# A four-layer graph network in one kernel: the way to the first tile reordered, two more lanes at the end, and two tanh as two steps

## The chip, the cores and the metric

The kernel runs on one core of one Trainium2 chip, in one launch. The metric is the device time of an execution in microseconds. Before the change three runs gave 5136.36 to 5138.56 us, with a median of 5137.93.

The core has five engines with a queue of instructions each: PE (TensorE, matrix products into PSUM), DVE (VectorE), ACT (ScalarE), POOL (GpSimd) and SP (SyncE, which here issues DMAs only). ACT's queue issues some DMAs too. [...]

## The reference

64 graphs of 256 nodes with 128 features pass through four layers. Every layer is `x = x + f(relu(layernorm(x)))`; the functions f are, cut to what is computed:

```python
# layer 0: attention of all pairs; W = adj cut into two halves of 128 columns
s1, s2 = h @ W1.T, h @ W2.T                                  # 256 values a node
pre = s1[:, :, None, :] + s2[:, None, :, :] + b_lin          # 64 x 256 x 256 x 256
e = einsum('bije,e->bij', where(pre >= 0, pre, 0.2 * pre), a) + adj
out = sigmoid(softmax(e, axis=2) @ h)
# layer 1: gated sum over neighbours
x_h = elu(h @ Wi + bi)
e = sigmoid(a_tgt[:, :, None] + a_src[:, None, :] + be) * mask(adj)
recv = elu(concat(e @ x_h, x_h * e.sum(-1)) @ Wn + bn)
out = concat(recv, x_h) @ Wm + bm
# layer 2: attention with tanh
A = exp(8 * tanh(h @ q @ (h @ k).T / sqrt(128) / 8)) * adj
out = (A / A.sum(-1)) @ h @ v
# layer 3: five steps of a gated recurrent unit
m = adj @ h                                                  # in and out matrix are both adj
z = sigmoid(concat(m, m) @ w3.T + b3 + h @ u3.T + bu)
r = sigmoid(concat(m, m) @ w4.T + b4 + h @ u3.T + bu)
hv = tanh(concat(m, m) @ w5.T + b5 + (r * h) @ u5.T + b)
h = (1 - z) * h + z * hv
```

The pair term of layer 0 is nearly all of the work: for each graph 256 x 256 pairs of 256 values are formed, passed through a leaky ReLU and summed with the weights a.

## The kernel before, in words

**Tiles.** The 64 graphs form 34 groups, `GROUPS = (1, 1) + (2,) * 30 + (1, 1)`: the first two and the last two groups hold one graph (width W = 256 columns), the others two (W = 512). Groups are counted from 0 here, so the last is 33.

**Layer 0.** `constants0` (L216) sorts the 256 channels by the sign of a: it counts signs with PE (`before`), computes places on DVE, builds the permutation `perm` (four DVE operations), and multiplies adj by it to get `w_p`, the permuted and scaled weights for s1 and s2. From the same pieces come `v2_rep`, `a_win`, `left2`, `left_w`, `adj_t`. `head` (L463) makes the layer norm of a group (`ln_relu`: DVE statistics, four POOL operations that end with `bsh`, two or four ACT operations), transposes it (`h0t`), and makes s1 and its negative s1n; `senders` (L512) makes s2 and, with a vector `bound` that takes a way through DRAM, the term `adj_l`.

The class `Pairs` (L538) then makes the pair tiles `r` of a graph: 32 rows by two channel halves by eight tiles of 128x256, so 512 tiles a graph. Three engines make them: ACT one tile at an instruction (L626), POOL one (L631), DVE four (L614). A batch of eight tiles is summed by PE into `e_ps` (L679) with four matmul instructions, which the trace shows as eight passes of 512 columns. If five batches already wait for PE, a row is "merged": DVE adds the second channel half into the first (L648), and PE gets one batch in place of two. Eleven buffers of r are shared by all. `softmax0` finishes the graph once its last batch is summed.

**Layers 1 to 3.** `layer1` (L759), `layer2` (L843) and `layer3` (L916) are generators: each `yield` ends a step and names the engine of the next. In layer 1 the two tanh of a graph (th_ps, L800) are issued in one step. A step of layer 3 is: `m_ps` (PE), copy to `m_t` (ACT), the products with u3 and w4 into `gate_ps`, tanh (r), `rh2` (DVE), the products with w34, w5 and u5, tanh of both sums (z and the candidate), three DVE operations to the new `hf`, a transpose (PE) and a copy to `hn` (ACT).

**What sets the order.** The order on every engine is written out by a planner while the program is built. A `Model` holds a clock for each engine, and every instruction adds a fixed cost to it. Pieces of work stand in chains (`ahead`, `behind`, `chain12` for layers 1 and 2, `chain3` and `chain4` for layer 3). A chain offers its next step at the latest of: its engine's clock, the end of its last step, a due time which grows by the chain's pace with each step (only while the planning is "paced"), and an earliest time that a step may name. The planner takes what can start first: a chain's step, a batch for PE, or an r tile. The chip's engines then follow these queues whatever their real times are. Layer 3 of groups 0 to 32 stands in `chain3`, one after the other; only the last group has its own lane, `chain4`, with PSUM banks that the pairs use earlier (`Home`, L899).

**The head of the program.** SP loads x of groups 0 and 1 and then most weights. ACT's queue issues adj_n, the columns of a and b_lin, and eight more small loads (L139), then its table load, then the first layer norm.

Of the kernel before, what the change touches and what calls it, by code (L numbers as in the profile page):

```python
# [12 lines left out]
P = 128  # L13
N = 256
# [7 lines left out]
MARGIN = {"pe": 300}  # L22
MEMORY = 7000
# [30 lines left out]
def kernel(ctx: ExitStack, tc: tile.TileContext, ins: dict, out: bass.AP):  # L54
# [87 lines left out]
    def column(name):  # L142

        v = ins[name]
        return fetch(
            [P, v.shape[0] // P], "c_" + name, v.rearrange("(c p) -> p c", p=P), nc.scalar
        )

    order = ctx.enter_context(tc.manual_schedule())
    xts = [load_x(0)]  # L150
    adj_n = fetch([P, 2, N], "adj_n", adj.rearrange("(c p) m -> p c m", p=P), nc.scalar)
    a_col = column("L0_gnn_a")
    blin = column("L0_gnn_b_lin")
    ident = constant([P, P], "ident")
# [47 lines left out]
    bm_bc = fetch([P, P], "bm_bc", ins["L1_gnn_bm"].partition_broadcast(P), nc.scalar)  # L202
    be_bc = fetch([P, 1], "be_bc", ins["L1_gnn_be"].partition_broadcast(P), nc.scalar)
# [12 lines left out]
    def constants0():  # L216
# [10 lines left out]
        yield "dve"  # L227
        sgn, a_abs = col("sgn"), col("a_abs")
        dve(2).tensor_scalar(sgn, a_col, 0.0, None, ALU.is_ge)
        dve(2).scalar_tensor_tensor(a_abs, a_col, -1.0, a_col, ALU.mult, ALU.max)  # L230
        for c in range(2):
            dve(P).tensor_scalar(
                a_rep[:, c, :], a_rep[:, c, :], a_col[:, c : c + 1], None, ALU.mult
            )
# [7 lines left out]


        v2_ps = psum([P, P], "v2_ps")
        for c in range(2):
            mm(
                v2_ps, lhsT=adj_n[:, c, P : 2 * P], rhs=a_rep[:, c, :],
                start=(c == 0), stop=(c == 1),
            )
        yield "dve"  # L250
        bef = constant([P, 3], "bef")
# [57 lines left out]
        odd_all = constant([P, 1], "odd_all")  # L309
        dve(1).tensor_copy(odd_all, p[:, 0:1])  # L310
# [150 lines left out]


# [49 lines left out]
    def senders(b, of, to):  # L512

        h_t = flat(of["h_t"][:, 2 * b : 2 * b + 2, :])
        yield "pe"
        p = psum_h([P, 2, N], "s2_ps")
        for ec in range(2):
            mm(p[:, ec, :], lhsT=w_p[:, 1, bass.ts(ec, P)], rhs=h_t, start=True, stop=True)
        yield "act"
        s2 = ap.tile([P, 2, N], F32, tag="s2", name="s2")  # L520
        act(2 * N).copy(s2, p)
        to["s2"] = s2
# [236 lines left out]
    def layer1(x1):  # L759
# [34 lines left out]
        for b in range(NB):  # L794
# [3 lines left out]
            yield "act"  # L798
            for jc in (1, 0):
                act(N, 1).activation(  # L800
# [379 lines left out]
```

## Time and profile before

| | |
|---|---|
| median of three runs | 5137.93 us |
| the profiled execution: its own time, its span | 5146.74, 5144.9 us |
| instructions of the profiled execution | 152945 |
| first r tile on ACT, last one ends | 23.84, 5033.99 us |
| end of the last batch of pairs (e_ps) | about 5043.2 us |
| first m_ps of the last group's layer 3 | 5097.22 us |
| last operation on DVE (y of the last group) ends | 5142.21 us |
| ACT's r tiles (L626) | 10460, six in 2.2 us |
| POOL's r tiles (L631) | 10200, 475 ns each, spaced 452 |
| DVE's r of four tiles (L614), merges (L648) | 1803, 4896 |
| matmul passes into e_ps (L679) | 27872 |

All times are from the span's start. The profile is of one execution, 8.8 us longer than the median. A table by stage has for each stretch the busy time of PE, PE's weight loads, DVE, ACT and POOL with their instructions in brackets, then the granted PE clock (1.00 is full), the DMA share and GB/s. In a timeline a row is start, duration, engine, line, operation, output<-input, shape and count, and in brackets the idle time before it with what ended it. In a list of waits a row is who waited for whom: total us, times, longest. Ends of matmuls are modelled: a row of PE reaches some 0.2 us past the point at which the next one starts.

### The profile page before, as it was taken

What the parts mean: (1) busy time and instruction counts of PE and PEld (TensorE: products, weight loads), DVE (VectorE), ACT (ScalarE), POOL (GpSimd) and SP (SyncE); (2) the same over time, 40 slices, a digit from 0 to 9 for tenths busy, and PEclk for the clock granted to TensorE, in tenths of its full rate; (3) what the DMA queues carried; (4) which work ended last, traced back from release to release, by engine and by line L of the source; (5) the groups of instructions that cost most, each with busy time, mean ns of one, the idle gap of its engine ahead of it and who ended that gap; (6) DMA issues with size and microseconds to landing.
All of it is one profiled execution on the core that took longest, in us unless ns stands there. A gap on an engine that the chain in (4) does not pass through costs nothing. (4 is left out here: it accounts for less than half of the span.)

```text
span 5144.9 us, 152945 instructions
## 1 busy us (share of the span) xinstructions
PE 5058.0 (98%) x57347; PEld 1988.1 (39%) x57347; DVE 4951.3 (96%) x9664; ACT 5034.1 (98%) x13196; POOL 4862.2 (95%) x10825
## 2 busy tenths in 40 slices
PE   8999999999999999999999999999999999999997
PEld 3334433334343343333344433333333334333343
DVE  7999999999999999999999999999999999999994
ACT  7999999999999999999999999999999999999994
POOL 8999999999999999999999999999999999999991
PEclk9999999999999999999999999999999999999999
DMA  0000000000000000000000000000000000000000
GB/s 20 6 2 5 5 6 6 4 4 6 6 6 6 2 6 6 6 6 2 6 6 6 6 2 6 6 6 6 2 6 6 6 6 5 2 5 4 4 6 6
DMA packets 56028, 28.10 MB, mean 5 GB/s; under 512 B 20337, under 2 KB 55281, under 8 KB 55281
## 3 DMA queue, kind: packets, MB, share of 16 engines
q1 hardware_dynamic: 53168, 17.97, 1.4%
q8 instruction: 449, 7.36, 0.6%
q14 instruction: 299, 2.44, 0.2%
q10 hardware_dynamic: 2112, 0.33, 0.0%
HBM read 9.84 MB, written 8.45 MB: 4 GB/s over the span
## 5 line engine op out<-in xcount | busy, mean ns | idle before, releaser
L631 POOL TENSOR_SCALAR r<-s,s1n 128x256 f32<-128x256 f32 x10200 | 4612.8, 475 | 81.0 <-PE e_ps L679 21.9
L626 ACT ACTIVATE r<-s_act,s 128x256 f32<-128x256 f32 x9948 | 4489.0, 1312 | 2.6 <-PE e_ps L679 2.6
L679 PE MATMUL e_ps<-r,a_win 128*32 128x512 f32 x27872 | 3330.9, 594 | 5.6 <-POOL r L631 2.3
L614 DVE TENSOR_TENSOR r<-s_dve,s1n 128x1024 f32<-128x1024 f32 x1803 | 2093.9, 1211 | 4.7
L648 DVE SCALAR_TENSOR_TENSOR r<-s_dve,s1n,r 128x256 f32<-128x256 f32 x4896 | 2002.3, 472 | 1.0 <-POOL r L631 1.0
L679 PEld LDWEIGHTS e_ps<-r,a_win 128*32 128x32 f32 x27872 | 958.1, 110 | 1734.4 <-issue 1255.6
L443 ACT ACTIVATE h<-x,bsh,brs 128x128 f32<-128x128 f32 x384 | 320.5, 1344 | 2.1 <-POOL bsh L437 2.1
L626 ACT ACTIVATE r<-s,s 128x256 f32<-128x256 f32 x512 | 311.1, 1207 | 0.0
L106 PE MATMUL m_ps<-adj_t,hn 128*32 128x256 f32 x4096 | 261.0, 388 | 3.1 <-ACT hn L974 3.0
L932 ACT COPY m_t<-m_ps 128x512 f32<-128x512 f32 (+1 forms) x170 | 229.4, 1349 | 15.8 <-PE m_ps L106 15.7
L951 ACT ACTIVATE gate_ps<-gate_ps,bz 128x512 f32<-128x512 f32 (+1 forms) x170 | 236.6, 1392 | 7.0 <-PE gate_ps L106 6.9
L953 ACT ACTIVATE hv_ps<-hv_ps,bh 128x512 f32<-128x512 f32 (+1 forms) x170 | 234.2, 1378 | 2.4 <-PE hv_ps L106 2.4
L938 ACT ACTIVATE m_ps<-gate_ps,br 128x512 f32<-128x512 f32 (+1 forms) x170 | 226.2, 1331 | 8.9 <-PE gate_ps L106 8.9
L974 ACT COPY hn<-hn_ps 128x512 f32<-128x512 f32 (+1 forms) x136 | 186.6, 1372 | 17.8 <-PE hn_ps L113 17.8
L106 PEld LDWEIGHTS m_ps<-adj_t,hn 128*32 128x32 f32 x4096 | 141.2, 112 | 132.0 <-issue 44.8
L106 PE MATMUL gate_ps<-m_t,t_w_w 128*32 128x512 f32 (+1 forms) x1360 | 173.3, 572 | 9.7 <-ACT m_t L932 9.0
L106 PE MATMUL gate_ps<-m_t,w_t 128*32 128x512 f32 (+1 forms) x1360 | 175.0, 569 | 5.0 <-ACT m_ps L938 5.0
L106 PE MATMUL hv_ps<-m_t,t_w_w 128*32 128x512 f32 (+1 forms) x1360 | 174.6, 567 | 0.0
L106 PE MATMUL hv_ps<-rh,u_th 128*32 128x512 f32 (+1 forms) x1360 | 174.5, 567 | 0.0
L432 POOL TENSOR_SCALAR bve<-bmv 128x4 f32<-128x4 f32 (+1 forms) x136 | 26.2, 193 | 128.7 <-DVE bmv L427 119.9
L106 PE MATMUL s_ps<-h0t,w_p 128*32 128x256 f32 (+1 forms) x1568 | 139.4, 449 | 5.4 <-ACT s1n L482 2.8
L106 PE MATMUL gate_ps<-hf,u_t 128*32 128x512 f32 (+1 forms) x1088 | 143.9, 574 | 0.0
(206 smaller groups left out, 5211.6 us busy)
## 6 DMA issues: line engine op xcount, KB each, us to landing
xt<-in_x_dram SPq DMA_DIRECT2D x30, 256.0 KB
out_dram<-y SPq DMA_DIRECT2D x30, 256.0 KB
row<-rows SPq DMA_DIRECT2D x128, 0.5 KB
xt<-in_x_dram SPq DMA_DIRECT2D x4, 128.0 KB
out_dram<-y SPq DMA_DIRECT2D x4, 128.0 KB
bound<-row SPq DMA_DIRECT2D x30, 2.0 KB
raw_L_gnn_w_w<-in_L_gnn_w_w_dram SPq DMA_DIRECT2D x3, 128.0 KB
adj_n<-in_adj_dram ACTq DMA_DIRECT2D x1, 256.0 KB
```

Source lines behind the costliest of these rows:

```text
L106: nc.tensor.matmul(out[bass.ts(c, 32), :], lhsT=lhsT[:, bass.ts(c, 32)], rhs=rhs, **flags)
L443: act(P, 2, 1).activation(h[:, g, :], xt[:, g, :], AF.Relu, bias=shift[:, g : g + 1], scale=rstd[:, g : g + 1],)
L614: nc.vector.tensor_tensor(r[:, 2 * g2 : 2 * g2 + 2, :, :], s2[:, ec : ec + 1, :].unsqueeze(1).to_broadcast([P, 2, 2, N]), self.s1n_v[:, ec ...
L626: nc.scalar.activation(r[:, g, ic, :], s2[:, ec, :], AF.Relu, bias=s1[:, ec, i : i + 1])
L631: nc.gpsimd.tensor_scalar(r[:, g, ic, :], s2[:, ec, :], FLT_MAX, s1n[:, ec, i : i + 1], ALU.min, ALU.max,)
L648: nc.vector.scalar_tensor_tensor(r[:, g, ic, :], self.own("dve")[:, 1, :], self.of["s1n"][:, 1, i : i + 1], r[:, g, ic, :], ALU.max, ALU.add,)
L679: nc.tensor.matmul(self.e_ps[bass.ts(g, 32), :, :].rearrange("p a b -> p (a b)"), lhsT=a_win[:, batch["ec"], 31 - t : 63 - t], rhs=flat(r[ ...
L932: act(W).copy(m_t, m_ps)
L938: act(W, 1).activation(t_r, g_ps, AF.Tanh, bias=br, scale=0.5)
L951: act(W, 1).activation(t_z, g_ps, AF.Tanh, bias=bz, scale=0.5)
L953: act(W, 1).activation(cand, hv_ps, AF.Tanh, bias=bh)
L974: act(W).copy(hn, tp)
```

## The change

**Head.** The column of a is ACT's first DMA and adj_n its second; all other columns, bm_bc and be_bc go to SP, b_lin as SP's second. A memset and a tanh on one element are put ahead of everything on DVE and ACT. In `constants0` the products that the first tile doesn't need (v2, a_rep, odd) move behind w_p; w_p's halves are made and copied one by one, the s2 half first; the products of b_lin come ahead of w_p's. The first group has its own head, `first_head`: s2 and s1 in one block of products, s1n on DVE, s1 on ACT. `constants0` and the first layer norm name an earliest time (LANDS).

**Planning.** The first graph isn't paced, and when its pairs begin, the planner's clocks are all set to at least ACT's.

**Layer 1.** Each of the two tanh of a graph is a step of its own, so that the planner may put other work between.

**End.** Group 32's layer 3 has the lane chain4, with the two banks that the last group had; group 33's has a new lane chain5 with three banks (two of e_ps, one of ps_h). Both may begin in the planning only when no pairs are left. In group 33 (`early`) the w5 product comes before the first tanh, u5 before w34, and the candidate's tanh before z's.

```diff
+LANDS = 3400
...
-    def column(name):
+    def column(name, queue=nc.sync):
         v = ins[name]
-        return fetch(
-            [P, v.shape[0] // P], "c_" + name, v.rearrange("(c p) -> p c", p=P), nc.scalar
-        )
+        return fetch([P, v.shape[0] // P], "c_" + name, v.rearrange("(c p) -> p c", p=P), queue)
...
     xts = [load_x(0)]
+    a_col = column("L0_gnn_a", nc.scalar)
     adj_n = fetch([P, 2, N], "adj_n", adj.rearrange("(c p) m -> p c m", p=P), nc.scalar)
-    a_col = column("L0_gnn_a")
     blin = column("L0_gnn_b_lin")
+    table = constant([P, 1], "table")
+    nc.vector.memset(table, 0.0)
+    nc.scalar.activation(table, table, AF.Tanh)
...
-    bm_bc = fetch([P, P], "bm_bc", ins["L1_gnn_bm"].partition_broadcast(P), nc.scalar)
-    be_bc = fetch([P, 1], "be_bc", ins["L1_gnn_be"].partition_broadcast(P), nc.scalar)
+    bm_bc = fetch([P, P], "bm_bc", ins["L1_gnn_bm"].partition_broadcast(P))
+    be_bc = fetch([P, 1], "be_bc", ins["L1_gnn_be"].partition_broadcast(P))
...
-        yield "dve"
+        yield "dve", None, LANDS + 500
         sgn, a_abs = col("sgn"), col("a_abs")
         dve(2).tensor_scalar(sgn, a_col, 0.0, None, ALU.is_ge)
-        dve(2).scalar_tensor_tensor(a_abs, a_col, -1.0, a_col, ALU.mult, ALU.max)
-        for c in range(2):
-            dve(P).tensor_scalar(
-                a_rep[:, c, :], a_rep[:, c, :], a_col[:, c : c + 1], None, ALU.mult
-            )
...
-        v2_ps = psum([P, P], "v2_ps")
-        for c in range(2):
-            mm(
-                v2_ps, lhsT=adj_n[:, c, P : 2 * P], rhs=a_rep[:, c, :],
-                start=(c == 0), stop=(c == 1),
-            )
-        yield "dve"
+        yield "dve"
+        dve(2).scalar_tensor_tensor(a_abs, a_col, -1.0, a_col, ALU.mult, ALU.max)
...
         yield "pe"
+        b_ps = psum([P, 2], "blin_ps")
+        for c in range(2):
+            for src in range(2):
+                mm(
+                    b_ps[:, c : c + 1], lhsT=perm[:, src, c, :], rhs=blin[:, src : src + 1],
+                    start=(src == 0), stop=(src == 1),
+                )
         p = psum([P, 2, N], "w_p_ps")
-        for half in range(2):
+        for half in (1, 0):
...
-        yield "act"
-        act(2 * N).copy(w_p, p)
-        counts["w_p"] += 1
+        yield "dve"
+        dve(2).tensor_copy(blin_p, b_ps)
+        dve(2).tensor_scalar(blin_n, b_ps, -1.0, None, ALU.mult)
+        for half in (1, 0):
+            yield "act"
+            act(N).copy(w_p[:, half, :], p[:, half, :])
+        counts["w_p"] += 2
+        yield "dve"
+        for c in range(2):
+            dve(P).tensor_scalar(
+                a_rep[:, c, :], a_rep[:, c, :], a_col[:, c : c + 1], None, ALU.mult
+            )
+        yield "pe"
+        v2_ps = psum([P, P], "v2_ps")
+        for c in range(2):
+            mm(
+                v2_ps, lhsT=adj_n[:, c, P : 2 * P], rhs=a_rep[:, c, :],
+                start=(c == 0), stop=(c == 1),
+            )
         yield "dve"
         dve(P).tensor_copy(v2_rep, v2_ps)
...
         yield "pe"
-        p = psum([P, 4], "odd_ps")
-        mm(p[:, 0:1], lhsT=ones, rhs=odd, start=True, stop=True)
-        for c in range(2):
-            for src in range(2):
-                mm(
-                    p[:, 1 + c : 2 + c], lhsT=perm[:, src, c, :], rhs=blin[:, src : src + 1],
-                    start=(src == 0), stop=(src == 1),
-                )
-        yield "dve"
-        dve(2).tensor_copy(blin_p, p[:, 1:3])
-        dve(2).tensor_scalar(blin_n, p[:, 1:3], -1.0, None, ALU.mult)
-        counts["w_p"] += 1
+        p = psum([P, 1], "odd_ps")
+        mm(p, lhsT=ones, rhs=odd, start=True, stop=True)
+        yield "dve"
...
-    def ln_relu(space, xt, tag, ln, when=None):
...
-                yield "dve", when
+                yield "dve", when, at
...
+    def first_head(xt, to, snd):
+        G, _, W = sizes(xt)
+        h = yield from ln_relu(ap, xt, "h0", "h0", at=LANDS)
+        h_t = yield from transpose_blocks(ap, h, "h0t", psum_h)
+        to.update(h=h, h_t=h_t)
+        yield "pe", lambda: counts["w_p"] > 1
+        s2_ps, s1_ps = psum_h([P, 2, N], "s2_ps"), psum_a([P, 2, W], "s1_ps")
+        for half, p in ((1, s2_ps), (0, s1_ps)):
+            for ec in range(2):
+                mm(
+                    p[:, ec, :], lhsT=w_p[:, half, bass.ts(ec, P)], rhs=flat(h_t),
+                    start=True, stop=True,
+                )
+        yield "dve"
+        s1n = ap.tile([P, 2, W], F32, tag="s1n", name="s1n")
+        for ec in range(2):
+            dve(W, 1).tensor_scalar(
+                s1n[:, ec, :], s1_ps[:, ec, :], -1.0, blin_n[:, ec : ec + 1], ALU.mult, ALU.add
+            )
+        yield "act"
+        s2 = ap.tile([P, 2, N], F32, tag="s2", name="s2")
+        act(2 * N).copy(s2, s2_ps)
+        s1 = ap.tile([P, 2, W], F32, tag="s1", name="s1")
+        for ec in range(2):
+            act(W, 1).activation(
+                s1[:, ec, :], s1_ps[:, ec, :], AF.Identity, bias=blin_p[:, ec : ec + 1]
+            )
+        to.update(s1=s1, s1n=s1n)
+        snd["s2"] = s2
...
+        if "s2" not in to:
+            yield "pe"
+            p = psum_h([P, 2, N], "s2_ps")
+            for ec in range(2):
+                mm(p[:, ec, :], lhsT=w_p[:, 1, bass.ts(ec, P)], rhs=h_t, start=True, stop=True)
+            yield "act"
+            s2 = ap.tile([P, 2, N], F32, tag="s2", name="s2")
+            act(2 * N).copy(s2, p)
+            to["s2"] = s2
...
-            yield "act"
             for jc in (1, 0):
+                yield "act"
                 act(N, 1).activation(
                     th_ps[:, jc, :], th_ps[:, 0, :], AF.Tanh,
                     bias=a_src[:, 2 * b + jc : 2 * b + jc + 1], scale=0.5,
...
-        def __init__(self, aside):
-            self.aside = aside
-        def bank(self, shape, name, odd):
-            if not self.aside:
+        LAST = ((ps_e, "e"), (ps_e, "e"), (ps_h, "ps_h"))
+        LAST_BUT_ONE = ((ps_d, "s2_dve"), (ps_c, "s2_act"))
+        def __init__(self, g):
+            self.banks = {len(GROUPS) - 1: self.LAST, len(GROUPS) - 2: self.LAST_BUT_ONE}.get(g)
+            self.taken = 0
+        def bank(self, shape, name):
+            if not self.banks:
                 return psum(shape, name)
-            space, tag = ((ps_d, "s2_dve"), (ps_c, "s2_act"))[odd % 2]
+            space, tag = self.banks[self.taken % len(self.banks)]
+            self.taken += 1
...
             act(W).copy(m_t, m_ps)
             yield "pe"
             mm(g_ps, lhsT=ws["w4_w"], rhs=m_t, start=False, stop=True)
+            early = home.banks is home.LAST
+            if early:
+                hv_ps = home.bank([P, W], "hv3_ps")
+                mm(hv_ps, lhsT=ws["w5_w"], rhs=m_t, start=True, stop=False)
...
             yield "pe"
+            if early:
+                mm(hv_ps, lhsT=u5_th, rhs=rh2, start=False, stop=True)
             mm(
                 g_ps, lhsT=w34_t, rhs=m_t, start=False, stop=True, skip_group_check=True
             )
-            hv_ps = home.bank([P, W], "hv3_ps", step)
-            mm(hv_ps, lhsT=ws["w5_w"], rhs=m_t, start=True, stop=False)
-            mm(hv_ps, lhsT=u5_th, rhs=rh2, start=False, stop=True)
-            yield "act"
+            if not early:
+                hv_ps = home.bank([P, W], "hv3_ps")
+                mm(hv_ps, lhsT=ws["w5_w"], rhs=m_t, start=True, stop=False)
+                mm(hv_ps, lhsT=u5_th, rhs=rh2, start=False, stop=True)
             t_z, cand = g_ps, hv_ps
-            act(W, 1).activation(t_z, g_ps, AF.Tanh, bias=bz, scale=0.5)
-            yield "act"
-            act(W, 1).activation(cand, hv_ps, AF.Tanh, bias=bh)
+            for of_z in (not early, early):
+                yield "act"
+                if of_z:
+                    act(W, 1).activation(t_z, g_ps, AF.Tanh, bias=bz, scale=0.5)
+                else:
+                    act(W, 1).activation(cand, hv_ps, AF.Tanh, bias=bh)
...
-        last = g == len(GROUPS) - 1
-        (chain4 if last else chain3).add(last_rest(g, x3, hn, h_t, Home(last)))
+        lane = {len(GROUPS) - 1: chain5, len(GROUPS) - 2: chain4}.get(g, chain3)
+        lane.add(last_rest(g, x3, hn, h_t, Home(g)))
     def last_rest(g, x3, hn, h_t, home):
+        if home.banks:
+            yield "pe", lambda: n == len(graphs) and not (making or doing or multiplying)
         y = yield from layer3(x3, hn, h_t, home)
         nc.sync.dma_start(out=of_group(out, g), in_=y)
         counts["out"] += 1
...
-    chain4 = Chain(2400)
-    chains = [ahead, behind, chain3, chain12, chain4]
+    chain4, chain5 = Chain(2400), Chain(2400)
+    chains = [ahead, behind, chain5, chain3, chain12, chain4]
...
-    ahead.add(head(xts[0], made[0]))
+    ahead.add(first_head(xts[0], made[0], sent[0]))
...
-        paced = n < len(graphs) - 2
+        paced = 0 < n < len(graphs) - 2
         if not making and n < len(graphs) and "s2" in sent[n]:
             g, b = graphs[n]
             making.append(Pairs(g, b, made[g], sent[n]))
+            if n == 0:
+                model.t = {e: max(t, model.t["act"]) for e, t in model.t.items()}
             multiplying.append(making[0])
```

More of the change, by code (lines that the diff above doesn't have):

```diff
@@ L296, in constants0 @@
         yield "pe"
-        p = psum([P, 4], "odd_ps")
-        mm(p[:, 0:1], lhsT=ones, rhs=odd, start=True, stop=True)
-        for c in range(2):
-            for src in range(2):
-                mm(
-                    p[:, 1 + c : 2 + c], lhsT=perm[:, src, c, :], rhs=blin[:, src : src + 1],
-                    start=(src == 0), stop=(src == 1),
-                )
+        p = psum([P, 1], "odd_ps")
+        mm(p, lhsT=ones, rhs=odd, start=True, stop=True)
         yield "dve"
-        dve(2).tensor_copy(blin_p, p[:, 1:3])
-        dve(2).tensor_scalar(blin_n, p[:, 1:3], -1.0, None, ALU.mult)
-        counts["w_p"] += 1
         odd_all = constant([P, 1], "odd_all")
-        dve(1).tensor_copy(odd_all, p[:, 0:1])
+        dve(1).tensor_copy(odd_all, p)
         left, left_n, left_nb = col("left"), col("left_n"), col("left_nb")
@@ L411, in constants1, with ln_relu @@
                 dve(1).tensor_scalar(t, t, scale, None, ALU.mult)
-    def ln_relu(space, xt, tag, ln, when=None):
+    def ln_relu(space, xt, tag, ln, when=None, at=None):
         G = xt.shape[1]
@@ L514, in senders @@
         h_t = flat(of["h_t"][:, 2 * b : 2 * b + 2, :])
[L515 to L518, printed above, removed]
-        yield "act"
-        s2 = ap.tile([P, 2, N], F32, tag="s2", name="s2")
-        act(2 * N).copy(s2, p)
-        to["s2"] = s2
+        if "s2" not in to:
[7 more added lines that the diff above has]
+            to["s2"] = s2
         if "bound" not in of:
@@ L899 @@
     class Home:
-        def __init__(self, aside):
-            self.aside = aside
-        def bank(self, shape, name, odd):
-            if not self.aside:
+        LAST = ((ps_e, "e"), (ps_e, "e"), (ps_h, "ps_h"))
[5 more added lines that the diff above has]
+            if not self.banks:
                 return psum(shape, name)
-            space, tag = ((ps_d, "s2_dve"), (ps_c, "s2_act"))[odd % 2]
+            space, tag = self.banks[self.taken % len(self.banks)]
+            self.taken += 1
             return space.tile(shape, F32, tag=tag, name=name)
         def tile(self, W, tag, name, bufs=1):
-            if not self.aside:
+            if not self.banks:
                 return bp.tile([P, W], F32, tag=tag, name=name, bufs=bufs)
@@ L920, in layer3 @@
             yield "pe"
-            m_ps = home.bank([P, W], "m_ps", step)
+            m_ps = home.bank([P, W], "m_ps")
             for b in range(NB):
@@ L927, in layer3 @@
                     )
-            g_ps = home.bank([P, W], "gate_ps", step + 1)
+            g_ps = home.bank([P, W], "gate_ps")
             mm(g_ps, lhsT=u3_t, rhs=hf, start=True, stop=False)
@@ L945, in layer3 @@
             )
-            hv_ps = home.bank([P, W], "hv3_ps", step)
-            mm(hv_ps, lhsT=ws["w5_w"], rhs=m_t, start=True, stop=False)
-            mm(hv_ps, lhsT=u5_th, rhs=rh2, start=False, stop=True)
-            yield "act"
+            if not early:
+                hv_ps = home.bank([P, W], "hv3_ps")
+                mm(hv_ps, lhsT=ws["w5_w"], rhs=m_t, start=True, stop=False)
+                mm(hv_ps, lhsT=u5_th, rhs=rh2, start=False, stop=True)
             t_z, cand = g_ps, hv_ps
-            act(W, 1).activation(t_z, g_ps, AF.Tanh, bias=bz, scale=0.5)
-            yield "act"
-            act(W, 1).activation(cand, hv_ps, AF.Tanh, bias=bh)
+            for of_z in (not early, early):
[4 more added lines that the diff above has]
+                    act(W, 1).activation(cand, hv_ps, AF.Tanh, bias=bh)
             yield "dve"
@@ L967, in layer3 @@
                 yield "pe"
-                tp = home.bank([P, W], "hn_ps", step)
+                tp = home.bank([P, W], "hn_ps")
                 turn()
@@ L976, in layer3 @@
         yield "pe"
-        tp = home.bank([P, W], "y_ps", step)
+        tp = home.bank([P, W], "y_ps")
         turn()
```

## The prediction, made before the changed kernel was run

> **What bounds the kernel now.** First the page's busy shares, then busy time by stage.
>
> ```profile
> PE 5058.0 (98%) x57347; PEld 1988.1 (39%) x57347; DVE 4951.3 (96%) x9664; ACT 5034.1 (98%) x13196; POOL 4862.2 (95%) x10825
> ```
>
> ```profile
> core 0: us, PE busy (x) PEld busy (x) DVE busy (x) ACT busy (x) POOL busy (x), PEclk, DMA share, GB/s
> 0.00:10.00 10.00, 1.61 (x56) 1.19 (x56) 5.29 (x30) 0.00 (x0) 3.07 (x17) 1.00 0.49 130
> 10.00:20.00 10.00, 5.81 (x90) 2.65 (x90) 1.35 (x10) 3.96 (x7) 0.00 (x0) 1.00 0.34 89
> ...
> 40.00:60.00 20.00, 17.71 (x131) 5.10 (x131) 16.82 (x37) 10.31 (x30) 19.65 (x44) 1.00 0.00 1
> ...
> 3000.00:4000.00 1000.00, 990.42 (x11112) 376.40 (x11108) 981.67 (x1950) 999.53 (x2617) 973.01 (x2161) 1.00 0.02 5
> ...
> 5100.00:5145.00 45.00, 30.94 (x442) 13.72 (x434) 15.43 (x37) 15.80 (x39) 0.00 (x0) 0.95 0.03 8
> ```
>
> The middle is full on four engines, and fullest on ACT: between 62 and 5030 us it idles 6.9 us. So the time is ACT's list from its first r to its last (23.84 to 5033.99), plus the head before, the idle time inside, and a tail of 110 us. What can move is at both ends. The head and the first graph, from the timeline and the waits between 23 and 62 us:
>
> ```profile
> 5.24 0.17 DVE L229 TENSOR_SCALAR sgn<-c_L_gnn_a 128x2 f32<-128x2 f32 x1 [0.85 <-DMA c_L_gnn_a<-in_L_gnn_a_dram]
> 10.49 1.28 ACT L443 ACT_TABLE_LOAD   x1 [10.49 <-DMA c_L_gnn_w_b<-in_L_gnn_w_b_dram]
> 13.12 3.64 PE L106 MATMUL w_p_ps<-perm,adj_n 128*32 128x256 f32 x32
> 23.84 1.71 ACT L626 ACTIVATE r<-s,s 128x256 f32<-128x256 f32 x4
> ```
>
> ```profile
> ACT h L443 <- POOL bsh L437: 9.7, 1, 9.7
> DVE adj_t L348 <- PE adj_t_ps L113: 7.6, 1, 7.6
> ACT rows L501 <- PE bound_ps L496: 5.1, 1, 5.1
> ```
>
> ACT issues ten DMAs until 10.45 before it loads its table; h comes at 11.79, and PE's w_p products stand behind h's transposes. Then ACT stops twice, 14.8 us in all, at instructions queued too early for PE and POOL. The tail, from PE's timeline (W = 256):
>
> ```profile
> 5115.61 1.07 PE L106 MATMUL m_ps<-adj_t,hn 128*32 128x256 f32 x16
> 5118.22 0.61 PE L106 MATMUL gate_ps<-m_t,t_w_w 128*32 128x256 f32 x8
> 5124.81 1.07 PE L106 MATMUL m_ps<-adj_t,hn 128*32 128x256 f32 x16
> 5133.64 1.81 PE L106 MATMUL m_ps<-adj_t,hn 128*32 128x256 f32 x16 [0.46 <-ACT hn L974]
> ```
>
> Two lanes of layer 3 alternate with a period of 9.20 us; no engine is full, latency sets the end.
>
> [...] granted clock 0.50 from 5052 to 5058, and 32 m_ps passes take 3.64 there against 1.91. [...]
>
> **Part 1, the way to the first tile.** Ten DMA issues leave ACT (0.33 to 0.49 us each) for SP. SP's list ended at 12.84, now near 17; its next use (row) is at 32.7, the next data needed from it (bm_bc) at DVE 47.0: hidden. The table load now runs near 1.7 to 3.0, before x lands (bst at 3.90). The new memset and one-element tanh (0.1 and about 0.2) hide there too.
> The column a: landed 4.0 us after its issue, behind the 256 KB of adj. Now first: earliest it is harmless (bst ends 4.39), latest 0.72 + 4.0 = 4.7. I take sgn at 4.45 (was 5.24). Then: PE's counts, 0.8 to bef (5.52 to 6.32), so bef 5.4; bef to the last perm, 2.8 (6.32 to 9.11), so 8.2 (adj_n, second on ACT, and blin, second on SP, are issued by 1.7 and have landed); blin product 0.5; w_p products 3.4 at the cold rate of the row above: 12.1. POOL's 1.4 us for rstd and h on ACT (0.88) end near 7.3, under that. The two transposes 0.6, h0t copy and its wait 0.6: 13.3. s products, 32 passes as one block, 1.9 warm (3.6 cold): 15.2. s1 by two ACTIVATEs 0.8, beside it s1n by two DVE operations (0.48 and 0.40, off ACT): first r on ACT and POOL at about 15.8, against 23.84: **-8.0**. Ends: -9.9 (a early, PE warm) to -6.0 (PE cold through s). DVE's first half comes later, after v_rep, a_win and s_dve, 17.7 against 24.57. The products for v2, odd, left and adj_t move behind the first tile; they were on the way only through PE's and DVE's order, and PE has room there (it waited 18.6 us for POOL's r between 23 and 62).
>
> **Part 2, the first graph's order.** The planner's four clocks are set equal at the first pair and the first graph isn't paced. In the changed program's queues ACT has 53 r before rows and 40 more before the next h (read from the order of the changed program's instructions on each engine); POOL has 71 r before that h's statistics. From 15.8, at 0.367 us an r on ACT (six in 2.2) and 0.4525 on POOL: POOL reaches bsh at 15.8+32.1+1.4 = 49.3, ACT reaches h at 15.8+35.5 = 51.3: no wait where 9.7 was. rows at 35.8; PE's bound product waits for DVE's left_w, about 36.4: 0.6 to 2.5 us where 5.1 was. adj_t's product, for which DVE stood 7.6, now stands behind 18 batches on PE and its copy behind 19 halves on DVE. I leave 2.3 of 14.8: **-12.5**, from -14 to -4 (an unforeseen stop of 10).
>
> **Part 3, the two tanh.** Same instructions; between them now stand mostly one to five r. ACT's r count is 10460 before and after, so its list is equally long: **0**. POOL has 20 r fewer, DVE 88 merges fewer and 27 halves more (-34.5+31.6 at 0.392 and 1.17), PE 11 batches more (+9.5 at 0.86): PE's passes at their measured rates (0.1075 for 512 columns) fill about 95% of the phase, so there is room. Bound: ACT idle from 3 less to 6 more.
>
> **Part 4, end of the pairs.** Before, 24 passes of the last batches stood behind group 31's transposes, m_ps and u3, and e_ps ended at 5043.2, 9.2 after ACT's last r. Now the last r come 2.0 after group 31's r-tanh, PE follows with w34, w5, u5 (2.6) and 40 passes (4.3), and group 31's next step starts after them: 5.5 to 7.2 after the last r: **-3**.
>
> **Part 5, tail.** From e_ps's end to the last group's first m_ps was 54.0 (5043.2 to 5097.2). Group 32's five steps now run in this stretch with group 31's last three. PE's list there is 20 (31) + 17 (32) + 10.5 (33) = 47.5 us warm, against about 33 plus 6.6 lost to the halved clock. Following the queues with the measured durations (us after e_ps's end, before in brackets): x1 8.4 (8.5); h_t's transposes 14.6 (15.7, cold); xh 19.6 (17.0), behind group 31's m_ps and u3; th 25.6 (22.0), behind its w34, w5, u5; rc 31.6 (30.2); x2 36.6 (34.9); g 42.6 (39.7), behind another such block; pm 47.3 (45.3); first m_ps 54.5 (54.0). Waits that this misses can add 2.5; I take 55. Then the last group is alone. A step: 9.20, less 1.1 (w4 behind the other lane, 5117.12 to 5118.22), less 1.0 (cand behind its hn copy), less 0.5 (u5 no longer behind w34 and w5): 6.6. [...] the last step before shows the price, w4 ends 3.5 instead of 2.0 after m_ps starts: 8.1 at worst, I take 7.4; the first step also waits for group 32's y, 8.0. Last step, y and output DMA: 10.1 (2.7 of it after y, as now). 55+8.0+3x7.4+10.1 = 95.3 against 101.7: **-6**, from -10 to 0.
>
> Sum: -8.0-12.5+0-3-6 = -29.5 on a span of 5144.9 (execution 5146.74, 8.8 above the median 5137.93): span 5115.4, median **5108**.
>
> **Rivals.**
> Tail gained nothing (13%): group 32's lane delays layers 1 and 2 of the last group to 58 and every step runs at the halved clock: 58+8.7+24.3+10.8 = 101.8. For it: PE's 47.5 of 55 us; against: three drops of clock in that stretch become rarer. -23.5: 5114.
> The first graph stalls elsewhere (10%): one in-order wait of 10 us, at rows or for an r buffer. For it: left_w now comes after 15 DVE halves; against: both queues worked out above. 5118.
> Better (10%): middle -3, warm steps, a early: 5098.
> Slower (3%): the single psum_a bank is held longer by the split tanh (up to five r, 1.8 us), and rsum or the next layer-1 product stops PE and then ACT in every graph. From 29.5/64 = 0.46 us a graph nothing is left; at 0.65 it is +12: 5150. Against: ACT idles 6.9 us in 62 graphs now, e_t made DVE wait only 9.0 in all.
> The parts don't do it (4%): a lands as late as before and the stops move: gain under 10.
> The forecast itself, 5102 to 5114: 60%.
> About 0.2% (10 us) can be told from no change. So faster 0.93, same 0.04, slower 0.03; range 5097 to 5121.
>
> **What would show it.** Table load before 3.5 and w_p products ahead of h's transposes; first r near 16; ACT busy over 90% from 20 to 60; POOL's bsh before ACT's h; ACT idle in the middle under 13 us; last r about 5013; e_ps's end within 7.5 us of it; last five steps at 6.6 to 8.1[...]. Wrong if s products run cold and a lands late, if rows stops ACT, or if e_t or rsum appear as waits in every graph.

## The result and the profile after

The changed kernel takes **5100.43 us** (median of six executions, 5098.04 to 5115.52), the kernel before beside it 5136.39 (six, 5134.57 to 5138.56): a ratio of **0.9934, 95% interval 0.9921 to 0.9947**, or 36 us less. Forecast were 5108 and a range of 5097 to 5121. The profiled execution is the slowest of the six: 5115.52, span 5112.6, against 5144.9 before.

Profiled executions of one kernel differ by some 10 us, 0.2% (an r starts 356.8 ns after the last in after and 356.1 in again, and the pairs take 4996.2 and 4985.9 us), so stretches are compared at one rate here: the profiles of before and after both have 356.8.

The page of the changed kernel, the line of busy shares:

```profile
PE 5042.1 (99%) x57435; PEld 1964.8 (38%) x57435; DVE 4950.0 (97%) x9606; ACT 5029.2 (98%) x13196; POOL 4876.0 (95%) x10805
```

Its busy time by stage (columns as before: stretch, its length, then PE, PEld, DVE, ACT, POOL, clock, DMA share, GB/s):

```profile
40.00:60.00 20.00, 19.86 (x170) 6.83 (x166) 19.93 (x30) 19.41 (x54) 18.34 (x41) 1.00 0.01 1
...
3000.00:4000.00 1000.00, 993.24 (x11316) 389.19 (x11312) 983.08 (x1914) 1000.00 (x2625) 978.20 (x2162) 1.00 0.02 5
```

The first graph is now as full as the middle: ACT has 19.41 of 20 us between 40 and 60, where it had 10.31. Its timeline at the head:

```profile
1.76 1.28 ACT L155 ACT_TABLE_LOAD   x1 [1.76 <-issue]
3.46 0.15 DVE L231 TENSOR_SCALAR sgn<-c_L_gnn_a 128x2 f32<-128x2 f32 x1
7.51 3.63 PE L107 MATMUL w_p_ps<-perm,adj_n 128*32 128x256 f32 x32
15.28 0.84 ACT L494 ACTIVATE s<-s_ps,blin_p 128x256 f32<-128x256 f32 x2 [1.25 <-DVE s1n L486]
16.01 1.70 ACT L664 ACTIVATE r<-s,s 128x256 f32<-128x256 f32 x4
```

The table load, the column a and the w_p products come first as worked out, and the first r starts at 16.01 instead of 23.84. The waits of ACT between 15 and 62 us (total, times, longest) have shrunk from 9.7 and 5.1 to this:

```profile
ACT s L494 <- DVE s1n L486: 1.2, 1, 1.2
ACT rows L538 <- PE bound_ps L533: 0.7, 2, 0.5
ACT h0t L465 <- PE h0t_ps L114: 0.3, 1, 0.3
```

PE's timeline of the last group's lone steps:

```profile
5067.54 1.07 PE L107 MATMUL m_ps<-adj_t,h 128*32 128x256 f32 x16
5075.85 1.93 PE L107 MATMUL m_ps<-adj_t,hn 128*32 128x256 f32 x16 [0.46 <-ACT hn L1027]
5084.50 1.86 PE L107 MATMUL m_ps<-adj_t,hn 128*32 128x256 f32 x16 [0.46 <-ACT hn L1027]
5093.00 1.93 PE L107 MATMUL m_ps<-adj_t,hn 128*32 128x256 f32 x16 [0.46 <-ACT hn L1027]
5101.60 1.90 PE L107 MATMUL m_ps<-adj_t,hn 128*32 128x256 f32 x16 [0.46 <-ACT hn L1027]
```

The period is 8.3 to 8.65 us where 7.4 was taken: four of the five m_ps run at half the clock (1.9 against 1.07; the granted clock is 0.68 on the mean from 5074 to 5106). In three stretches the two profiles stand so; "pairs" runs from ACT's first r to the last pass into e_ps, "tail" from there to the end of the span:

| us | before | after | predicted for after |
|---|---|---|---|
| first r on ACT | 23.84 | 16.01 | 15.8 |
| pairs | 5019.5 | 4996.2 | 5004 |
| tail | 101.6 | 100.4 | 95.3 |

The pairs gained 23 where 15.5 were forecast (parts 2, 3 and 4 together), the tail 1 where 6 were. Two questions for the chip: what made the extra 8 us, and is the tail really worth nothing?

### The profile page after: what moved, and what is told of

It reads as the page before. It is cut to its first block, busy times and chain, and to the rows that moved or that the text cites. A ratio compares the mean times of both kernels' runs of the same rounds, so it can differ in the third digit from the quotient of the medians.

```text
span 5112.6 us, 153009 instructions
## 1 busy us (share of the span) xinstructions
PE 5042.1 (99%) x57435; PEld 1964.8 (38%) x57435; DVE 4950.0 (97%) x9606; ACT 5029.2 (98%) x13196; POOL 4876.0 (95%) x10805
## 5 line engine op out<-in xcount | busy, mean ns | idle before, releaser
L664 ACT ACTIVATE r<-s_act,s 128x256 f32<-128x256 f32 x9948 | 4611.6, 1577 | 0.9 <-PE e_ps L717 0.8
L686 DVE SCALAR_TENSOR_TENSOR r<-s_dve,s1n,r 128x256 f32<-128x256 f32 x4808 | 1964.2, 472 | 0.5 <-ACT r L664 0.4
L664 ACT ACTIVATE r<-s,s 128x256 f32<-128x256 f32 x512 | 365.4, 1609 | 0.0
L1006 ACT ACTIVATE hv_ps<-hv_ps,bh 128x512 f32<-128x512 f32 (+1 forms) x170 | 278.2, 1636 | 9.1 <-PE hv_ps L107 9.1
L1004 ACT ACTIVATE gate_ps<-gate_ps,bz 128x512 f32<-128x512 f32 (+1 forms) x170 | 281.8, 1658 | 4.0 <-PE gate_ps L107 4.0
L976 ACT COPY m_t<-m_ps 128x512 f32<-128x512 f32 (+1 forms) x170 | 270.5, 1591 | 13.5 <-PE m_ps L107 13.3
L986 ACT ACTIVATE m_ps<-gate_ps,br 128x512 f32<-128x512 f32 (+1 forms) x170 | 267.7, 1575 | 9.6 <-PE gate_ps L107 9.4
L838 ACT ACTIVATE th_ps<-th_ps,a_src 128x256 f32<-128x256 f32 x128 | 202.5, 1582 | 1.5 <-PE th_ps L107 1.5
L107 PE MATMUL gate_ps<-m_t,t_w_w 128*32 128x512 f32 (+1 forms) x1360 | 176.5, 578 | 10.3 <-ACT m_t L976 9.2
L741 ACT ACTIVATE pm<-e_ps,nmax 128x256 f32<-128x256 f32 x128 | 185.1, 1446 | 0.5 <-DVE nmax L732 0.5
L771 ACT ACTIVATE e_ps<-e_ps,rh 128x128 f32<-128x128 f32 x128 | 166.6, 1302 | 0.2 <-PE e_ps L107 0.2
```

Source lines behind the costliest of these rows:

```text
L107: nc.tensor.matmul(out[bass.ts(c, 32), :], lhsT=lhsT[:, bass.ts(c, 32)], rhs=rhs, **flags)
L664: nc.scalar.activation(r[:, g, ic, :], s2[:, ec, :], AF.Relu, bias=s1[:, ec, i : i + 1])
L686: nc.vector.scalar_tensor_tensor(r[:, g, ic, :], self.own("dve")[:, 1, :], self.of["s1n"][:, 1, i : i + 1], r[:, g, ic, :], ALU.max, ALU.add,)
L976: act(W).copy(m_t, m_ps)
L986: act(W, 1).activation(t_r, g_ps, AF.Tanh, bias=br, scale=0.5)
L1004: act(W, 1).activation(t_z, g_ps, AF.Tanh, bias=bz, scale=0.5)
```

## The experiments

Each run is compared with the kernel before in the same set of runs (5146.3, 5146.4 and 5146.5 us in the three sets, each on a chip of its own: again to split_alone, warm to act_dmas, plan_off to rates).

| run | median us | ratio to before, 95% | first r | pairs | tail |
|---|---|---|---|---|---|
| again | 5107.5 | 0.992 [0.9907, 0.9934] | 15.80 | 4985.9 * | 93.7 * |
| join | 5117.1 | 0.994 [0.9926, 0.9953] | 15.51 | 5004.5 | 99.8 |
| pair_l2 | 5119.1 | 0.9948 [0.9935, 0.996] | 16.15 | 5006.1 | 95.0 |
| split_alone | 5135.4 | 0.9978 [0.997, 0.9986] | 23.91 | 5008.6 | 102.5 |
| warm | 5106.3 | 0.9919 [0.9905, 0.9932] | 16.35 | 4986.5 * | 93.5 * |
| lanes_old | 5116.1 | 0.9938 [0.9925, 0.995] | 15.76 | 4985.8 * | 102.6 * |
| clocks_old | 5105.8 | 0.9917 [0.9904, 0.9931] | 16.03 | 4985.3 * | 94.0 * |
| act_dmas | 5112.0 | 0.993 [0.9917, 0.9944] | 16.13 | 4996.1 | 97.2 |
| plan_off | 5113.3 | 0.9936 [0.9924, 0.9949] | 15.65 | 4997.8 | 99.0 |
| both | 5107.3 | 0.9924 [0.991, 0.9938] | 15.92 | 4996.1 | 93.4 |
| rates_act | 5066.9 | 0.9846 [0.9832, 0.9859] | 16.22 | 4953.0 | 96.4 |
| rates | 5078.9 | 0.987 [0.9856, 0.9883] | 15.90 | 4974.0 | 87.6 |

The columns from "first r" on are of the profiled execution. A star marks 356.1 ns a r; times 1.002, 4985.9 is 4996.0, the value of after. With that the pairs of after, again, warm, act_dmas and both, which have the same queues there but for the first microseconds, agree within 0.7 us, so differences of some 1 us and more can be read.

### What the split of the two tanh is worth

Between before and after ACT's number of r is the same (10460), so its instructions should take equally long. They don't, and a view that the prediction didn't use says where. The groups of ACT's instructions by line and form give, behind the bar, busy time and the mean length of one record in ns. The kernel before:

```profile
L626 ACT ACTIVATE r<-s_act,s 128x256 f32<-128x256 f32 x9948 | 4489.0, 1312 | 2.6 <-PE e_ps L679 2.6
L800 ACT ACTIVATE th_ps<-th_ps,a_src 128x256 f32<-128x256 f32 x128 | 98.0, 766 | 2.6 <-PE th_ps L106 0.4
```

The changed kernel:

```profile
L664 ACT ACTIVATE r<-s_act,s 128x256 f32<-128x256 f32 x9948 | 4611.6, 1577 | 0.9 <-PE e_ps L717 0.8
L838 ACT ACTIVATE th_ps<-th_ps,a_src 128x256 f32<-128x256 f32 x128 | 202.5, 1582 | 1.5 <-PE th_ps L107 1.5
```

An r's record is 1312 or 1577 ns long though r start 357 ns apart: the records overlap, up to eight at a time in both traces. A tanh of before has 766 on the mean, because half of them have 450, near the shortest tanh of all (433). That is the second of each pair. It writes the half of th_ps that the first reads, and the semaphore that it waits on is ACT's own: in all 64 pairs it starts 32 to 34 ns after the first one's end, and in these 32 to 34 ns no record of ACT is under way. The timeline of the kernel before shows one place:

```profile
1799.62 0.95 ACT L800 ACTIVATE th_ps<-th_ps,a_src 128x256 f32<-128x256 f32 x2
1800.48 0.83 ACT L626 ACTIVATE r<-s_act,s 128x256 f32<-128x256 f32 x2
```

0.86 us from the first tanh to the r behind the second, where two starts take 0.71. By the ends, which count when starts bunch, the second tanh of a pair ends 482 ns (median) after the first in the kernel before; in the changed kernel a tanh ends 339 ns after the instruction ahead of it. 64 x 0.143 = 9 us. Of each 0.143 only 0.033 is idle time in the profile: the first tanh's record runs until just before the second starts.

Theory A is this; its rival B is that the planner's other order made the 8 us. Three kernels beside the changed one, on one chip:

```diff
 # join: the changed kernel, with
             for jc in (1, 0):
-                yield "act"
                 act(N, 1).activation(
+            # (one yield "act" ahead of the loop, as before)
 # pair_l2: the changed kernel, with
             act(2 * N, table=1).activation(s_ps, s_ps, AF.Tanh, scale=INV_SQRT_D / 8.0)
-            yield "act"
             act(2 * N, table=1).activation(s_ps, s_ps, AF.Exp, scale=8.0)
 # split_alone: the kernel before, with the two lines of the split and nothing else
```

> The changed kernel once more, as the measure for the runs beside it. Both theories: 5098 to 5102 us, 36 under the kernel before; ACT from its first to its last r 4989 us; second tanh of a graph ends 0.34 us after the instruction before it.

> The changed kernel with layer 1's two tanh of a graph as one step again. Theory A (the second tanh overwrites what the first reads, so ACT waits for its own first tanh to end[...]: in the kernel before the second ends 0.482 us after the first, in the changed kernel 0.339 after the instruction ahead of it): 64 x 0.143 = 9 us slower than the changed kernel, about 5109; the ACT phase from first to last r 9 us longer, and all of it in the step from the first tanh to the second. Theory B (the 7 us that the middle gained come from the planner's different order, the split itself is worth nothing, as predicted): within 3 us of the changed kernel, of either sign, and no such step in the ends.

> The changed kernel with layer 2's tanh and exp of a graph (both in place on the same PSUM tile) put one right behind the other, where r stood between them. Theory A: another 64 dependent pairs[...]: 64 x 0.14 = 9 us slower than the changed kernel, the exp ending about 0.63 us after the tanh where it took 0.487. Theory B: within 3 us, either sign.

> The kernel before with the two tanh as two steps, and nothing else of the change. Theory A: 9 us faster than the kernel before, about 5127, ACT from first to last r 5001 instead of 5010. Theory B: within 3 us of the kernel before.

Measured: join is 9.5 us slower than the changed kernel beside it, pair_l2 11.6 slower, and split_alone 10.9 faster than the kernel before, with an interval that leaves 1 out. The intervals of join and again overlap a little; the pairs at one rate don't leave the question open, with 5004.5 in join against 4996.2. The tanh in join and in split_alone:

```profile
L838 ACT ACTIVATE th_ps<-th_ps,a_src 128x256 f32<-128x256 f32 x128 | 103.5, 809 | 2.8 <-PE th_ps L107 0.7
L800 ACT ACTIVATE th_ps<-th_ps,a_src 128x256 f32<-128x256 f32 x128 | 196.8, 1538 | 1.5 <-PE th_ps L106 1.5
```

Up to ACT's last r, the sum over the ends into the tanh is 51.9 us in join and 43.0 in the changed kernel (52.0 before, 43.3 in split_alone), so the step itself is worth 8.7 to 8.9. The stretch from ACT's first to its last r moved by less than the 9 us expected: 7.5 more in join, 6.4 less in split_alone (5010.1 to 5003.7). In split_alone another 4.5 of the 10.9 come after the last r, where e_ps ends 4.9 us behind it in place of 9.4; so the step is shown, but that the totals come so near to 9 is partly luck. The layer-2 pair, which was never part of the change, shows the same mark. pair_l2:

```profile
L909 ACT ACTIVATE s_ps<-s_ps 128x512 f32<-128x512 f32 x64 | 78.0, 1219 | 0.5 <-PE s_ps L107 0.5
L910 ACT ACTIVATE s_ps<-s_ps 128x512 f32<-128x512 f32 x64 | 37.2, 582 | 2.0
```

and the changed kernel, where r stand between the two:

```profile
L911 ACT ACTIVATE s_ps<-s_ps 128x512 f32<-128x512 f32 x64 | 97.7, 1527 | 0.0
```

The exp's record falls to 582 ns, its end comes 614 ns (median) behind the tanh's instead of 487, and the sum of these steps grows by 8.0 us. Theory A is confirmed by taking the split away, by adding it alone, and by the same fault made elsewhere; B expected under 3. Of pair_l2's 11.6 some 3 are not explained by it; ACT also has 8 r more there (10468), an estimated 2.9 us at 0.365 each.

### What the tail is worth: the clock

again, the changed kernel once more, had a tail of 93.7 us. PE's timeline there:

```profile
5057.03 1.07 PE L107 MATMUL m_ps<-adj_t,h 128*32 128x256 f32 x16
5065.08 1.07 PE L107 MATMUL m_ps<-adj_t,hn 128*32 128x256 f32 x16 [0.46 <-ACT hn L1027]
5071.99 1.07 PE L107 MATMUL m_ps<-adj_t,hn 128*32 128x256 f32 x16 [0.46 <-ACT hn L1027]
5078.89 1.07 PE L107 MATMUL m_ps<-adj_t,hn 128*32 128x256 f32 x16 [0.46 <-ACT hn L1027]
```

Same queues, steps of 6.9 us. Up to the first m_ps, 55.3 us behind e_ps in both, the two tails agree within 0.02 us; what differs is the granted clock, 0.68 from 5074 to 5090 in after and 1.00 in again. Is it a cause, or does it follow? Within a step ACT's and DVE's records have the same length in both traces (0.37 and 0.45, 0.42 us). From m_ps to rh, where PE's products ran at half the clock (m_ps 1.86 against 1.07), the slow step of 5084.50 takes 4.15 us and the fast one of 5071.99 takes 2.80; from rh to the next hn 3.92 and 3.68. So the time is lost in PE's own products, 1.35 us of it. warm puts products into the gaps: PE stands idle for 1.7 us before a transpose in after and again:

```diff
             if early:
+                for _ in range(3):       # behind w34; one more between w5 and u5
+                    mm(psum([P, W], "warm"), lhsT=ones, rhs=m_t, start=True, stop=True)
```

> The changed kernel with four idle matmuls of 128x256 in each step of the last group (one between w5 and u5, three behind w34; their results are read by nobody). Theory A (the five lone steps take 8.6 us where PE's clock drops in the gap of 1.7 us before the transposes, and 6.9 where it doesn't, as two executions of the changed kernel show): clock 1.0 to the end, steps of 6.9 us, tail 93 to 94 us in every execution, 3 to 4 us under the changed kernel's median and 7 under its execution with a tail of 100.4. Theory B (the steps are latency of ACT and DVE, and the clock only follows): tail unchanged or longer by up to 2 us, since the idle matmuls stand ahead of u5 and of the transposes.

In after the granted clock fell four times in these steps, twice in such a gap (5074.39 and 5091.45) and twice 0.1 us behind the start of m_ps (5084.63 and 5101.69).

The same view of warm:

```profile
5066.20 1.07 PE L107 MATMUL m_ps<-adj_t,hn 128*32 128x256 f32 x16 [0.46 <-ACT hn L1031]
5073.05 1.07 PE L107 MATMUL m_ps<-adj_t,hn 128*32 128x256 f32 x16 [0.46 <-ACT hn L1031]
5079.89 1.07 PE L107 MATMUL m_ps<-adj_t,hn 128*32 128x256 f32 x16 [0.46 <-ACT hn L1031]
```

Steps of 6.85 us with the idle matmuls in them, 0.30 us of idle time before a transpose, and a tail of 93.5 here and of 93.4 in both, at the other rate. Since again reached 93.7 without them, one such trace proves little; the count over all traces says more. Of the last four m_ps of the last group 11 of 28 ran at half the clock, for part of their length at least, in the seven traces with these lanes and no idle matmuls (after 4, again 0, join 3, pair_l2 1, clocks_old 0, act_dmas 2, plan_off 1), and 1 of 16 in the four with them. That one is in rates_act, so "in every execution" was too much:

```profile
5034.13 1.94 PE L107 MATMUL m_ps<-adj_t,hn 128*32 128x256 f32 x16 [0.46 <-ACT hn L1032]
5042.26 1.07 PE L107 MATMUL m_ps<-adj_t,hn 128*32 128x256 f32 x16 [0.46 <-ACT hn L1032]
```

B, that the clock only follows, is out by the comparison within the step. Of the 3 to 4 us that A expected in the median about 1 is seen, less than the intervals can tell: what the idle matmuls save in time is not shown.

What the lane itself gives:

```diff
-        lane = {len(GROUPS) - 1: chain5, len(GROUPS) - 2: chain4}.get(g, chain3)
+        last = g == len(GROUPS) - 1        # Home, layer3 and last_rest as before
+        (chain4 if last else chain3).add(last_rest(g, x3, hn, h_t, Home(last)))
```

> The changed kernel with layer 3 of the last two groups as before: group 32 back in the common lane behind group 31, the last group's banks, its order of w5, u5, w34 and of its two tanh as before, no wait for the end of the pairs. Theory A (the prediction's parts 4 and 5 are worth 9 us): 9 us slower than the changed kernel, steps of 9.2 us, tail 101 to 102, last r to the end of e_ps 9 us. Theory B (the lane gains only what the two profiles show, 2.6 + 1.1): 3 to 4 us slower.

Its PE, two lanes taking turns again at 9.2 us:

```profile
5063.22 1.07 PE L107 MATMUL m_ps<-adj_t,hn 128*32 128x256 f32 x16 [0.46 <-ACT hn L1012]
5065.86 1.07 PE L107 MATMUL m_ps<-adj_t,hn 128*32 128x256 f32 x16
5072.42 1.07 PE L107 MATMUL m_ps<-adj_t,hn 128*32 128x256 f32 x16 [0.46 <-ACT hn L1012]
5075.06 1.07 PE L107 MATMUL m_ps<-adj_t,hn 128*32 128x256 f32 x16
```

30.3 us under before where again, in another set, is 38.8 under it: 8.5 us slower, tail 102.6 against 93.7 at the same rate. Against the tail of 100.4, with the clock down, it would be 2.2. Theory A in size, but not in place: from the last r to the end of e_ps it takes 6.78 us in both. The lane earns all in the tail; part 4's 2.6 come from elsewhere in the order.

### What the head and the first graph's plan are worth

```diff
 # clocks_old: the changed kernel, with
-            if n == 0:
-                model.t = {e: max(t, model.t["act"]) for e, t in model.t.items()}
 # plan_off: that, and
-        paced = 0 < n < len(graphs) - 2
+        paced = n < len(graphs) - 2
```

> The changed kernel without the line that sets the planner's four clocks equal at the first pair; the first graph stays unpaced. POOL then has 89 r before the next group's statistics where it had 71, ACT 94 before that h where it had 89. Theory A (ACT's stops in the first graph come from such an order): POOL's bsh at 15.4 + 89 x 0.4525 + 1.4 = 57.1, ACT at h by 16.0 + 94 x 0.365 + 0.8 = 51.1, so ACT stands 6 us at h, and the kernel is 6 to 7 us slower. Theory B (pacing alone made those stops, or ACT makes them good later): under 2 us slower.

> The changed kernel without its two edits of the first graph's plan: the four clocks aren't set equal, and the first graph is paced. (The first product on e_ps is held until v2_rep is made, since nothing else holds it then.) In its queues ACT has 44 r ahead of rows and 41 more ahead of h, POOL 86 r ahead of that h's statistics; ACT has 10440 r in all, 20 fewer than the changed kernel. Theory A (time is ACT's list plus its stops, and the stops of the kernel before came from where the constants stood, not from these two edits): ACT stops about 8 us at h and 1 at rows, 20 r x 0.365 = 7.3 us of list fall away, the kernel is within 3 us of the changed one. Theory B (the prediction's part 2, the two edits are worth 12.5 us): 10 to 13 us slower.

clocks_old ran like the changed kernel, 40.6 us under before. Its stop was made, 5.9 us of it, but 5.3 of that at rows and 0.6 at h. It has 16 r fewer on ACT, 5.8 us of list, and the two cancel. plan_off, waits of ACT between 15 and 62 us:

```profile
ACT rows L539 <- PE bound_ps L534: 5.5, 2, 5.3
ACT r L665 <- PE e_ps L718: 2.1, 1, 2.1
...
ACT h L450 <- POOL bsh L444: 0.6, 1, 0.6
```

ACT stops for 8.2 us where the changed kernel stops for 1.0 and the kernel before for 14.8, 20 r (7.3 us) have left ACT, and the pairs take 1.6 us longer: ACT's stretch from first to last r is 5.3 shorter, but e_ps ends 13.7 us after the last r in place of 6.8. Its median is about 6 us above again's, outside both expectations; the pairs explain 1.6, and its tail of 99.0 had the halved clock. In both runs the stop at h that I had computed from POOL's queue shrank to 0.6, since ACT came 5 us late to it through rows.

So the two edits of the plan take away about 7 of the 13.7 us of stops, and yet are worth only about 2 us in the pairs, since the plan without them gives ACT less to do. By subtraction the new order at the head is left with some 11: between split_alone (5008.6) and the changed kernel (4996.2) the pairs lose 12.4, of which the two edits are 1.6 and the lanes nothing (lanes_old has 4996 at the same rate). The head's order was not undone on its own, so its share is not shown.

```diff
 # act_dmas: the changed kernel, with
-    def column(name, queue=nc.sync):
+    def column(name, queue=nc.scalar):     # bm, be on nc.scalar too, the table's tanh behind
```

> The changed kernel with nine DMA issues back on ACT's queue, and the tanh that loads the table behind them; a stays first on that queue, and the order of the constants stays. Theory A (ACT's issue list and PE's order both held the first tile, the issue list on its own only by what h ends later than the w_p products): table load near 10, h 11.3 to 12.2, its transposes at 12.2 instead of 11.1, first r 1.0 to 1.6 us later than the 16.0 of the changed kernel, and the kernel as much slower. Theory B (the issue list is the whole of part 1): first r 6 to 8 us later.

Its timeline:

```profile
8.88 1.28 ACT L207 ACT_TABLE_LOAD   x1 [8.88 <-DMA c_L_gnn_w_b<-in_L_gnn_w_b_dram]
...
10.28 0.86 ACT L449 ACTIVATE h<-xt,bsh,brs 128x128 f32<-128x128 f32 x2
...
11.09 0.69 PE L114 MATMUL h0t_ps<-ident,h 128*128 128x128 f32 x2
```

The transposes of h start at 11.09, in the changed kernel at 11.08: they stand behind the w_p products, which end there. First r 16.13 instead of 16.01, pairs the same to 0.1 us. Both theories expected more. The nine issues on ACT cost 0.1 us once a and the w_p products come first; the 4 us in the median are not in the head (the tail was 97.2, with two of its m_ps at half the clock).

### s1 behind s1n, and a better kernel

```diff
 # both: warm, and each half of s1's product in a PSUM tile of its own
+        s1_ps = (psum_a([P, W], "s1_ps"), ps_c.tile([P, W], F32, tag="s2_act", name="s1_ps"))
 # rates_act: both, and          rates: that, and HALF = 1170
-    TILE = {"act": 357, "pool": 453}
+    TILE = {"act": 365, "pool": 453}
```

> The changed kernel with the idle matmuls of the earlier run, and with the two halves of the first s1 product in two PSUM banks, so that ACT's s1 and VectorE's s1n of a half don't meet in one tile. Theory A (s1 waits 1.25 us for s1n because both read one tile): the wait falls to under 0.5, first r at 15.2 instead of 16.0, tail 93.5: 3 us under the changed kernel. Theory B (s1 waits for something else of VectorE, blin_p for one): first r unchanged, only the tail's 2 us.

> The run with both, and the planner's time for one r on ACT set from 357 to 365 ns, which is what an r takes by the ends in every trace. ACT has 10284 r instead of 10460, POOL 28 more, VectorE 85 halves more and 192 merges fewer, PE 24 batches more. Theory A (time is ACT's list plus its stops, and the others have room): 176 x 0.365 = 64 us less on ACT, of which VectorE (24 us more on 98 per cent) and POOL (13 more) leave 15 to 30: 15 to 30 us faster. Theory B (all four are full, and ACT's stops take the place of its r): within 5 us of the run with both, with ACT's stops up by 50 us or more.

> The run with both, and the planner's times set to what the traces show on two engines: r on ACT 365 ns instead of 357, a half on VectorE 1170 instead of 1131. ACT has 108 r fewer, POOL 96 more, VectorE 91 halves more and 352 merges fewer, PE 44 batches more. Theory A: ACT's list 39 us shorter, VectorE's 32, POOL's 43 longer, so that POOL, with 98 per cent, becomes the bound and the gain ends at 10 to 25 us. Theory B: within 5 us of the run with both.

The wait of 1.25 us stayed. The timeline of both:

```profile
14.22 0.87 DVE L487 TENSOR_SCALAR s1n<-s_ps,blin_n 128x256 f32<-128x256 f32 x2 [5.89 <-PE s_ps L107]
15.19 0.84 ACT L495 ACTIVATE s<-s_ps,blin_p 128x256 f32<-128x256 f32 x2 [1.25 <-DVE s1n L487]
```

It isn't blin_p, which DVE had ended at 7.9. But the experiment doesn't tell the rest apart: DVE took the halves in the order 1, 0 and ACT in 0, 1, so ACT's first half was DVE's last, and a wait from tile to tile would look the same as one for both. In the changed kernel, with one tile and both engines in the order 0, 1, ACT's first half waited for DVE's second as well. Open.

The planner counts 357 ns for an r on ACT, while by the ends an r takes 365 (median). The idea was that ACT so gets too many. With 365 it has 10284 r, and the kernel takes **5066.9 us, 40 us less than with both and 80 less than before**. Page of rates_act:

```profile
PE 5028.1 (99%) x57787; PEld 1979.7 (39%) x57787; DVE 4959.5 (98%) x9499; ACT 4972.6 (98%) x13020; POOL 4884.9 (96%) x10833
```

176 r of 0.365 are 64 us of list; the pairs fall by 43. I had expected 15 to 30: the other engines took up more than I allowed for. rates, with DVE's half also at its measured length, gives POOL 96 r more and gains 28, where 10 to 25 were expected and 12 us less than rates_act. So truer costs are not of themselves the better plan: that fewer r on ACT is faster is shown, that 365 is the best value is not.

## Why the prediction was right, and where it was not

**Part 1** (-8.0; -7.8). The instants hold, and w_p, 3.63 us, was the chain. Two steps in it failed without changing the sum. "s1 by two ACTIVATEs, beside it s1n": they ran one behind the other, which cost 1.25 us, about what the early a (sgn at 3.46, not 4.45) had won; that the sum holds so closely is partly luck. And of the ten DMA issues that leave ACT, putting nine back costs 0.1. Whether the transfers themselves take as long from SP's queue was not tested.

**Part 2** (-12.5; ACT's stops fell by 13.7). The size is right, from both queues, with some luck: POOL ended bsh at 51.14, not 49.3, and ACT came to h at 51.25, so of 2.0 us of room 0.1 was left. The cause is right only in part: with the equal clocks and the missing pace both undone, 7 us of stops come back, but the pairs lose only 1.6 us. That the planner, with other edits, also shares out the r otherwise was not in the sum.

**Part 3** (0; about -9). Of the whole prediction this is the step that failed: "ACT's r count is 10460 before and after, so its list is equally long". The count of instructions left out that one of them waits for the one ahead of it. In the kernel before the second tanh did so once in each graph, 0.143 us each time by the ends, and join and split_alone show it at 9.5 and 10.9 us. The profile of before had it in sight (766 ns among records of 1312).

**Part 4** (-3; -2.6) is right in size, and in its order: after w34, w5 and u5 PE ends with 40 passes, 6.8 us after the last r. The lane has no share in it, and where layer 3's products fall there moves this end by microseconds (4.9 in split_alone, 13.7 in plan_off).

**Part 5** (-6; -1.2 in the profiled execution, -7.8 in the other at its own rate). The road to the first m_ps was right within 0.5 us (55.3 against 55). The step of 7.4 us was a mean of two states of the clock: a step is 6.9 where the clock holds (1.00 in again), and 7.7 (act_dmas, pair_l2) to 8.65 where it drops (0.68 in after). Rival 1, "tail gained nothing", is what the profiled execution shows, and not what the median suggests; lanes_old puts the lane at 8.5.

The forecast of 5108 was 8 us too high, about part 3's 9; the rest of its sum holds, though in part 5 only where the clock holds. **Slower**, through th_ps held longer, did not come: DVE waits for th_ps 1.3 us in all, three times.

## What to carry to other kernels

Here a record much shorter than its neighbours of the same size (450 ns among 1312) marked an instruction that waited for the one right ahead of it on its own engine. Look for such a pair, compare the ends (482 ns against 339 here), and try unrelated work between the two. The length alone is no proof: in rates_act r's records have 829 ns on the mean and in both 1578, though an r ends 365 after the last in each. If a planner shares out the work, vary its costs early: 2% on one engine's tile was worth 40 us, as much as the whole change. In plan_off ACT stopped for 8.2 us where the changed kernel stops for 1.0, and the pairs took 1.6 longer, with 20 r fewer on ACT: count instructions by engine before adding stops up.

## What the runs showed that was not expected

**When the clock fell.** In the traces of before and after every recorded stretch of one granted clock between two changes is a multiple of 3.41 us long, the shortest 3.41. PE's busy time was summed in each 3.41 us of before from 5041.68 and of after from 5009.54 on. At full clock, eight had 0.41 to 1.41 us of work, and half clock followed each; 37 had 1.96 or more, and full clock followed each; of four with 1.53 to 1.62, half clock followed two. At half clock, full clock followed the eight with 2.95 us or more, and half clock the three with 2.53 to 2.70. PE was not idle ahead of the fall at 5052 in the kernel before: it had 1.08 us of work there. A lone step of 6.9 us is about two times 3.41; that it keeps or loses the clock by where these stretches fall is an estimate from these figures, not shown. PE's ends are modelled, so the figures hold to some hundredths.

**The uniform rate.** Over the pairs the profiled execution of after fell behind that of again, with the same queues, by 10.3 us of 4996.2, or 0.2%, the same share as an r's 356.8 ns and 356.1. The first execution of again was as much shorter than its others (5097.22 against 5106.33 to 5111.80), which fits. What sets it wasn't tried.
